# Two attention layers: one head of a pair turned on TensorE instead of by DMA, averages two steps behind their scores

## The chip, the cores and the metric

The kernel runs on one core of a Trainium2 chip. The metric is the device time of one execution in microseconds (us). One core has five engines with instruction streams of their own: PE (TensorE, matrix products), DVE (VectorE), ACT (ScalarE), POOL (GpSimd) and SP (SyncE, which here only issues DMAs). They meet through semaphores. SBUF is the on-chip memory, PSUM the memory of eight banks that PE writes its results to; DRAM is off the core and is reached by DMA.

## What is computed

The input x holds 8 batches of 512 tokens of 256 numbers, f32. Four layers follow, each with a layer norm ahead and added to x:

```
x = x + attention_a(layernorm(x))   # 16 heads of 64, causal, linear bias by distance (alibi), bias on the output
x = x + experts(layernorm(x))       # f1: 8 experts, the best 2 of each token, swiglu
x = x + attention_b(layernorm(x))   # 8 heads of 128, causal, rotary positions
x = x + experts(layernorm(x))       # f2: the same weights as f1
```

Attention is the usual one: scores S = q kT, softmax by rows, then the average of v with the rows of the softmax, and the output projection. In layer b the scores are divided by 128.

```python
sim = jnp.einsum('bhid,bhjd->bhij', q, k) + rel * slopes      # layer a
sim = jnp.where(causal, mask_value, sim)
attn = jax.nn.softmax(sim, axis=-1)
out = jnp.einsum('bhij,bhjd->bhid', attn, v)
return out.reshape(b, n, HEADS * DIM_HEAD) @ w_out + b_out
```

## The kernel before

The order of the whole program is: layer a, expert layer f1, layer b, expert layer f2. Each layer of attention has 64 *steps* (b, g), 8 batches by 8. In layer a a step is a pair of heads (i = 0 and 1, 64 rows of the array each); in layer b it is one head of 128. Tokens are cut in four tiles of 128, and since attention is causal a head's scores are ten blocks of 128x128 (tile `it` of the queries against tiles `jt` up to `it`), which lie packed in one buffer S of 1280 columns (`PACKED`); the layout of the blocks is `S_AT`.

What a step does, with the names that profile rows carry:

- `project` (L334): q (j = 0) and k (j = 1) of the *next* step, on PE, `pp`. In layer a ACT copies q and DVE copies k out of PSUM into `qk`. In layer b positions are rotated: three operations on DVE (`rot`, `rot`, `qk`, L353 to L355) and an add on POOL (L356).
- `scores` (L362): q kT on PE into PSUM, `sp`, in three groups of tiles (n = 0, 1, 2); DVE adds the bias or mask and finds each row's maximum (L413), ACT takes the exponential and its sums (L423). S is left in SBUF. In layer a POOL prepares the two heads' biases, `ali` (L382).
- `send` (L435), right after the last scores: the rows are scaled by 1/sum (L447, on DVE or POOL). The average needs S with keys on the partitions, so S is turned by DMA. The DMA's transpose works on 16-bit numbers: the f32 words are first taken apart in two planes of halves, `apart` (two copies, L450 to L454, on ACT or POOL), these go to DRAM, `away` (640 KB, L456), and a transposing DMA brings them back as `PT` (L460). All of these DMAs are issued from SP's queue.
- `values` (its matmuls are L325): v of two heads at a time, in the even steps, in two pieces `vp`; ACT copies them.
- `average` (L466): the turned blocks against v on PE, `op`, 12 matmuls for each head. It reads `PT`, so it waits for the transpose. Its result goes to `O` (DVE in layer a, ACT in b).
- `project_out` (L498): the output projection of four steps' `O`, `yp`, two pieces in step 5 and two in step 1 of the next batch; DVE adds to x.

`step` (L513) sets the order of these on PE. In layer a: scores 0, 1, 2 of the current step, q of the next step, extras 1, k of the next step, extras 2, then the average of the step before. In layer b: scores 0, q of the next step, scores 1 and 2, k of the next step, extras 1 and 2, then the average of the step before. The extras (L1151 to L1177) are the values, the output projections and small parts of the next layers: the norms (`xn`, `hn`), their transposes on PE (`xtp`, L282), and the gates and counts of the experts (`lp`, `cp`). They fall on fixed g: values on even g, output projections on 1 and 5, the transposes for the expert layer on 3 and for the next batch on 6; g 7 has none.

PE's instructions run in the order in which the program writes them (a manual schedule, L125). The other engines' orders are chosen by the framework's planner. Buffers come from rotating pools, which set who must wait: S has 3 buffers, `PT` 2, `apart` 2, `qk` 3, `tmp` (`ali` and `rot`) 2, the eight PSUM banks are one pool `ps`. `PT`, `apart`, `xT` and S buffers are used again by the expert layers, for gathered rows (`g_f`, L930), activations (L991) and for rows to be added (`collect`, L1105).

Between layers: `layer` (L1141) hands back the work that is left when the 64 steps are done: the average of step 63, the last output projections and the last norm. `flush` (L1195) places these pieces between the first blocks of the expert layer, at the block numbers of `turns`. An expert block is a gather by indirect DMA from POOL's queue (L937), four transposes (`gtp`), the two products (`hp`, `y`) and a scatter (L1041).

Of the kernel before, what the change touches and what calls it, by code (L numbers as in the profile page):

```python
# [49 lines left out]
P = 128  # L50
NB, T, D = 8, 512, 256
NT = T // P
# [15 lines left out]
S_BANKS = [(3,), (2, 0), (1,)]  # L68
BLOCKS_ROW = 10
PACKED = BLOCKS_ROW * P  # L70

AVERAGE = [((0, 1), 0), ((1,), 1), ((2, 3), 0), ((2, 3), 1), ((2, 3), 2), ((3,), 3)]

# [25 lines left out]
def layers(  # L99
# [187 lines left out]
    class Attention:  # L287
# [147 lines left out]
        def send(self, b, g):  # L435

            kind, nh = self.kind, self.nh

            last = (b, g) == (NB - 1, NQ - 1)
            sent = []  # L440
            for i, (S, nm, sums) in enumerate(self.S.pop((b, g))):
                key = f"{kind}_{b}_{g}_{i}"
                nc.vector.reciprocal(sums, sums)
                for it in (3, 2, 0, 1):
                    s = S[:, S_AT[it] * P : (S_AT[it] + it + 1) * P]
                    eng = nc.vector if it == 3 or i == 1 or last else nc.gpsimd
                    eng.tensor_scalar(s, s, sums[:, it : it + 1], 1.0, ALU.mult, ALU.mult)  # L447
                halves = S.bitcast(U16).rearrange("p (w s) -> p s w", s=2)
                apart = work.tile([P, 2, PACKED], U16, tag="apart", name=f"apart_{key}")
                nc.scalar.copy(apart[:, 0, :], halves[:, 0, :])  # L450
                if i == 1 and not last:
                    nc.gpsimd.tensor_copy(apart[:, 1, :], halves[:, 1, :])
                else:
                    nc.scalar.copy(apart[:, 1, :], halves[:, 1, :])  # L454
                away = dram.tile([P, 2, PACKED], U16, tag="away", bufs=4, name=f"away_{key}")
                nc.sync.dma_start(out=away, in_=apart)  # L456
                sent.append(away)
            for i, away in enumerate(sent):
                PT = work.tile([P, PACKED], F32, tag="PT", name=f"PT_{kind}_{b}_{g}_{i}")
                nc.sync.dma_start_transpose(  # L460
                    out=PT.bitcast(U16).rearrange("p (n w) -> p n w", n=BLOCKS_ROW),
                    in_=away.rearrange("p s w -> (p s) w"),
                )
                self.PT[b, g, i] = PT

        def average(self, b, g):  # L466
            kind, nh = self.kind, self.nh
            key = f"{kind}_{b}_{g}"
            PT = [self.PT.pop((b, g, i)) for i in range(nh)]
            if g % HALF == 0:  # L470
                self.O[b] = work.tile(
                    [P, HALF, T], F32, tag="O", bufs=1, name=f"O_{kind}_{b}_{g}"
                )
            v = self.V[b, g // 2]
            op = ps.tile([P, T], F32, tag="ps", bufs=8, name=f"op_{key}")
            cols = P // nh
            for its, jt in AVERAGE:
                n = len(its)
                first = S_AT[its[0]] + jt
                step = S_AT[its[-1]] - S_AT[its[0]] if n > 1 else 1  # L480
                for i in range(nh):
                    c0 = (g % 2) * P + i * cols
                    rows = PT[i].rearrange("p (n w) -> p n w", n=BLOCKS_ROW)
                    nc.tensor.matmul(  # L484
                        op[i * cols : (i + 1) * cols, its[0] * P : (its[-1] + 1) * P].rearrange(
                            "p (n w) -> p n w", n=n
                        ),
                        lhsT=v[:, jt, c0 : c0 + cols],
                        rhs=rows[:, first : first + step * (n - 1) + 1 : step, :],
                        start=(jt == 0),  # L490
                        stop=(jt == its[-1]),
                    )
            if kind == "a":
                nc.vector.tensor_copy(self.O[b][:, g % HALF, :], op)  # L494
            else:
                nc.scalar.copy(self.O[b][:, g % HALF, :], op)
# [13 lines left out]
                    )  # L510
                nc.vector.tensor_tensor(X[b][:, t, :], yp[:, 0:D], X[b][:, t, :], ALU.add)

        def step(self, last, cur, after, extra):  # L513

            there = set(self.qk)

            def project(j):
                if after and (*after, j) not in there:
                    self.project(*after, j)

            self.scores(*cur, 0)
            if self.kind == "a":
                self.scores(*cur, 1)
                self.scores(*cur, 2)
                project(0)
                extra(1)
                project(1)
                extra(2)
            else:
                project(0)  # L530
                self.scores(*cur, 1)
                self.scores(*cur, 2)
                project(1)
                extra(1)
                extra(2)
            if last:
                self.average(*last)


    class Experts:  # L540
# [389 lines left out]
        def gather(self, i, j):  # L930
            m = FIRST[i] + j
            if m % ROWS == 0:
                tag = "apart" if m else "xT"
                self.rows[m // ROWS] = work.tile(
                    [P, ROWS, D], F32, tag=tag, name=f"g_{self.kind}_{m}"
                )
            nc.gpsimd.indirect_dma_start(  # L937
                out=self.rows[m // ROWS][:, m % ROWS, :],
                out_offset=None,
                in_=self.h_all[0 : STAGES[i][1] * T, :],  # L940
                in_offset=bass.IndirectOffsetOnAxis(ap=self.R["token"][i][:, j : j + 1], axis=0),
            )
# [30 lines left out]
        def first(self, i, j):  # L973
# [17 lines left out]
            m = FIRST[i] + j  # L991
            if self.followed and m >= TOTAL - 5:
                if m == TOTAL - 5:
                    self.ended = work.tile([P, 5, FI], F32, tag="PT", name=f"a_{key}")
                a = self.ended[:, m - TOTAL + 5, :]
            else:
                if m % 2 == 0:
                    self.acts = work.tile([P, 2, FI], F32, tag="qk", bufs=3, name=f"a_{key}")
                a = self.acts[:, m % 2, :]
# [105 lines left out]
        def collect(self, b, tiles, tag, engines):  # L1105

            m = b * NT + tiles[0]
            bufs = {"S": 3, "xT": 2, "PT": 2, "apart": 2}[tag]
            got = work.tile(
                [P, 2, len(tiles), D],  # L1110
                F32,
                tag=tag,
                bufs=bufs,
                name=f"yg_{self.kind}_{b}_{tiles[0]}",
            )
            for k in range(2):
                self.read(engines[k], b, got[:, k], k * PLANE + m * P, len(tiles) * P)
            self.got[b, tiles[0]] = got
# [22 lines left out]
    def layer(att, exp, more):  # L1141
# [38 lines left out]
        for n, cur in enumerate(steps):  # L1180
            def extra(k, cur=cur):
                for piece in todo.get((*cur, k), ()):
                    piece()

            att.step(
                steps[n - 1] if n else None,
                cur,
                steps[n + 1] if n + 1 < len(steps) else None,
                extra,
            )  # L1190
        last = steps[-1]

        return [lambda: att.average(*last)] + left

    def flush(left, exp):  # L1195

        turns = (6, 6, 6, 7, 9, 12, 14, 16, 18)
        aside = {}
        for n, piece in zip(turns, left, strict=True):
            aside.setdefault(n, []).append(piece)  # L1200
        for n, piece in zip((20, 22, 24, 26, 29, 32), exp.sorting(1), strict=True):
            aside[n] = [piece]
        return aside
# [17 lines left out]
    aside = flush(layer(att_a, exp_a, more), exp_a)  # L1221
    aside.setdefault(8, []).append(weights_b)
    aside[done] = [lambda: exp_a.fetch(0)]
    for k, tag in enumerate(("xT", "PT")):
        tt = (2 * k, 2 * k + 1)
        aside[done].append(lambda tt=tt, tag=tag: exp_a.collect(0, tt, tag, both_queues))
        aside[done + 3 + k] = [lambda tt=tt: exp_a.add(0, tt)]
# [28 lines left out]
    halves = [(b, tt) for b in range(*STAGES[0]) for tt in ((0, 1), (2, 3))]  # L1256
    for k, (b, tt) in enumerate(halves):
        n = done + 3 * k // 2
        tag = ("xT", "PT")[k % 2] if k not in (8, 9) else "apart"
        aside.setdefault(n, []).append(  # L1260
            lambda b=b, tt=tt, tag=tag: exp_b.collect(b, tt, tag, both_queues)
        )
        aside.setdefault(n + 4, []).append(lambda b=b, tt=tt: exp_b.add(b, tt))
        aside.setdefault(n + 6, []).append(lambda b=b, tt=tt: store(b, tt, nc.sync))
# [1 line left out]
    exp_b.run(aside)  # L1266
    last = [(b, tt) for b in range(*STAGES[1]) for tt in ((0, 1), (2, 3))]
    for k, (b, tt) in enumerate(last):
        exp_b.collect(b, tt, "S" if k < 3 else "apart", (nc.sync, nc.scalar))
    for m in range(end, n + 7):  # L1270
        for piece in aside.get(m, ()):
            piece()
# [69 lines left out]
```

## Time and profile before

| what | value |
|---|---|
| median of 3 runs | 2282.01 us (2281.39 to 2282.07) |
| profiled execution | 2285.09 us |
| its span in the profile | 2283.0 us |
| mean granted clock of PE | 0.964 |
| instructions | 31747 |
| layer a | 16 to about 930 us |
| expert layer f1 alone | about 937 to 1190 us |
| layer b | about 1190 to 2015 us |
| expert layer f2 and the end | to 2283 us |
| DMA queue of SP | 319.28 MB, 51.6% of the 16 DMA engines' span |

The profile is of one execution, 3.1 us slower than the median of the runs, which carry no profiler's records. In its rows "L484 PE MATMUL op_a<-PT_a,V_a x24" means: line 484, engine PE, writes `op_a`, reads `PT_a` and `V_a`, 24 instructions; a bracket at the end says how long the engine was idle just before and what ended it. SPq is the queue of SP. The granted clock of PE is 1.00 at full speed; where it is 0.5 for a stretch, matmuls take twice as long.

### The profile page before, as it was taken

The page shows a single profiled execution, that of the slowest core. Times are in us where ns is not written, and L with a number is a line of the kernel's source. Part 1 is how long each engine was busy: PE and PEld are TensorE (multiplying, and loading weights), DVE is VectorE, ACT ScalarE, POOL GpSimd, SP SyncE. Part 2 cuts the span into 40 slices and gives each one's busy share as a digit, 9 for nine tenths or more (in the row PEclk, how much of TensorE's full clock was granted, in tenths as well). Part 3 has the DMA queues.
Part 4 walks back from the last instruction along what each step waited for, and adds up shares of the span by engine and source line. Part 5 has one row for each costly group of instructions (what it writes and reads, how often), then busy time and mean ns, then how long its engine had stood idle before and what let it go on. Part 6 is the DMA issues. An engine that isn't in the chain of part 4 may idle for free.

```text
span 2283.0 us, 31747 instructions
## 1 busy us (share of the span) xinstructions
PE 2064.2 (90%) x9329; PEld 1332.0 (58%) x9329; DVE 1615.2 (71%) x4943; ACT 1120.8 (49%) x2593; POOL 958.8 (42%) x1211
## 2 busy tenths in 40 slices
PE   6898999999999999799998999999999998989995
PEld 3555555555555555455655666666666665655663
DVE  3466767676767688477676676777677778867768
ACT  3566666666666666323324444444444444432331
POOL 4343434343434333366643343333334333345662
PEclk8999999999999999899999999999999999999998
DMA  9877777878777878732224444454535443452237
GB/s 297 237 191 206 194 205 195 212 195 211 187 212 192 215 182 233 180 109 79 84 77 118 113 141 118 125 144 115 149 105 149 110 135 93 134 147 95 84 100 248
DMA packets 603689, 360.37 MB, mean 158 GB/s; under 512 B 510304, under 2 KB 564736, under 8 KB 603520
## 3 DMA queue, kind: packets, MB, share of 16 engines
q1 hardware_dynamic: 587968, 319.28, 51.6%
q0 software_dynamic: 13632, 37.24, 5.2%
q10 hardware_dynamic: 1920, 1.84, 0.3%
q8 instruction: 77, 1.26, 0.2%
q14 instruction: 92, 0.75, 0.1%
HBM read 67.02 MB, written 165.43 MB: 102 GB/s over the span
## 4 chain that ended last, share of the span: by engine, by line
PE 44%; DVE 8%; DMA 4%; POOL 1%; issue 1%; SPq 1%; ACT 0%; DVEq 0%; another core or an unknown queue 0%; POOLq 0%; ACTq 0%
PE hp_f L980 9%; PE pp_b L343 8%; PE op_b L484 6%; PE sp_b L401 5%; PE yp_b L504 5%; PE y_f L1029 4%; PE vp_b L325 3%; DMA PT_b<-away_b 2%; PE gtp_f L951 1%; PE atp_f L1015 1%; DVE rot_b L354 1%; DVE rot_b L353 1%; DVE S_b L413 1%; DVE qk_b L355 1%; DVE u_f L1001 1%
## 5 line engine op out<-in xcount | busy, mean ns | idle before, releaser
L423 ACT ACTIVATE S_a<-S_a,nm_a 128x512 f32<-128x512 f32 (+3 forms) x512 | 281.0, 552 | 241.1 <-DVE nm_a L413 241.0
L356 POOL TENSOR_TENSOR qk_b<-qk_b,rot_b 128x512 f32<-128x512 f32 x128 | 168.8, 1319 | 394.1 <-DVE qk_b L355 369.8
L484 PE MATMUL op_a<-PT_a,V_a 128*64 128x256 f32 (+1 forms) x1536 | 197.0, 385 | 82.7 <-DMA PT_a<-away_a 79.0
L382 POOL TENSOR_SCALAR ali_a<-alibi 128x512 f32<-128x512 f32 x128 | 79.2, 621 | 433.4 <-DVE nm_a L413 412.8
L423 ACT ACTIVATE S_b<-S_b,nm_b 128x512 f32<-128x512 f32 (+3 forms) x256 | 142.0, 556 | 228.8 <-DVE nm_b L413 228.8
L980 PE MATMUL hp_f<-we,hT_f 128*128 x512 | 246.3, 604 | 7.2 <-DVE u_f L1001 5.8
L413 DVE CUSTOM_DVE_ANT_0 S_a<-sp_a,ali_a 128x512 f32<-128x512 f32 (+3 forms) x512 | 216.7, 487 | 29.9 <-PE sp_a L401 26.8
L484 PEld LDWEIGHTS op_a<-PT_a,V_a 128*64 128x64 f32 x1536 | 122.1, 151 | 169.0 <-DMA PT_a<-away_a 63.8
L484 PE MATMUL op_b<-PT_b,V_b 128*128 128x256 f32 (+1 forms) x768 | 166.5, 371 | 45.6 <-DMA PT_b<-away_b 45.6
L413 DVE CUSTOM_DVE_ANT_0 S_b<-sp_b,mask 128x512 f32<-128x512 f32 (+3 forms) x256 | 115.0, 486 | 127.7 <-PE sp_b L401 127.6
L1041 POOL DMA_INDIRECT y_f<-y_f,row_f x142 | 142.8, 1006 | 144.1 <-DVE y_f L1040 89.7
L450 ACT COPY apart_a<-S_a 128x1280 uint16<-128x1280 uint16 x128 | 161.0, 1258 | 83.6 <-POOL S_a L447 81.1
L1002 ACT ACTIVATE u_f<-u_f 128x256 f32<-128x256 f32 x142 | 59.4, 418 | 266.1 <-DVE u_f L1001 182.0
L484 PEld LDWEIGHTS op_b<-PT_b,V_b 128*128 128x128 f32 x768 | 144.9, 206 | 74.6 <-issue 40.0
L401 PE MATMUL sp_b<-qk_b,qk_b 128*128 128x512 f32 (+3 forms) x512 | 162.1, 440 | 17.3 <-POOL qk_b L356 17.3
L937 POOL DMA_INDIRECT g_f<-h_all_f,token_f x142 | 141.9, 999 | 78.6 <-issue 38.3
L1001 DVE TENSOR_TENSOR u_f<-hp_f,be 128x512 f32<-128x512 f32 x142 | 98.2, 691 | 98.1 <-PE hp_f L980 35.6
L494 DVE COPY O_a<-op_a 128x512 f32<-128x512 f32 x64 | 44.1, 689 | 172.7 <-PE op_a L484 172.6
L401 PE MATMUL sp_a<-qk_a,qk_a 64*128 64x512 f32 (+3 forms) x1024 | 157.8, 447 | 7.0 <-DVE qk_a L360 6.8
L1029 PEld LDWEIGHTS y_f<-we,aT_f 128*128 128x128 f32 x568 | 108.0, 192 | 78.5 <-issue 60.5
L1029 PE MATMUL y_f<-we,aT_f 128*128 x568 | 147.7, 383 | 4.2 <-ACT aT_f L1020 4.0
L447 DVE TENSOR_SCALAR S_a<-S_a,sum_a 128x512 f32<-128x512 f32 (+3 forms) x323 | 141.5, 487 | 4.1
(204 smaller groups left out, 4446.9 us busy)
## 6 DMA issues: line engine op xcount, KB each, us to landing
away_a<-apart_a SPq DMA_DIRECT2D x128, 640.0 KB
away_b<-apart_b SPq DMA_DIRECT2D x64, 640.0 KB
h_all_f<-hn_f SPq DMA_DIRECT2D x64, 128.0 KB
xm_f<-x_mid_f SPq DMA_DIRECT2D x16, 512.0 KB
yg_f<-y_f SPq DMA_DIRECT2D x32, 256.0 KB
yg_f<-y_f SPq DMA_DIRECT2D x56, 128.0 KB
we<-w_dram SPq DMA_DIRECT2D x8, 512.0 KB
x_mid_f<-x SPq DMA_DIRECT2D x8, 512.0 KB
```

Of the source, the lines that this page charges most:

```text
L343: nc.tensor.matmul(pp, lhsT=w[:, c, g * P : (g + 1) * P], rhs=self.xT[b][:, c, :], start=(c == 0), stop=(c == NC - 1),)
L356: nc.gpsimd.tensor_tensor(qk, qk, rot, ALU.add)
L401: nc.tensor.matmul(sp[i][:, at[it] : at[it] + w], lhsT=q[r, it * P : (it + 1) * P], rhs=k[r, 0:w], start=True, stop=True,)
L413: nc.vector.tensor_tensor_reduce(out=s, in0=sp[i][:, at[it] : at[it] + w], in1=add[i][:, T - w : T], scale=scale, scalar=float(np.finfo(np ...
L423: nc.scalar.activation(s, s, AF.Exp, bias=nm[:, it : it + 1], scale=-1.0, accum_out=sums[:, it : it + 1],)
L447: eng.tensor_scalar(s, s, sums[:, it : it + 1], 1.0, ALU.mult, ALU.mult)
L450: nc.scalar.copy(apart[:, 0, :], halves[:, 0, :])
L484: nc.tensor.matmul(op[i * cols : (i + 1) * cols, its[0] * P : (its[-1] + 1) * P].rearrange("p (n w) -> p n w", n=n), lhsT=v[:, jt, c0 : c0 ...
L937: nc.gpsimd.indirect_dma_start(out=self.rows[m // ROWS][:, m % ROWS, :], out_offset=None, in_=self.h_all[0 : STAGES[i][1] * T, :], in_offs ...
L980: nc.tensor.matmul(hp, lhsT=h[:, c * P : (c + 1) * P], rhs=we_sb[:, bass.DynSlice(wat + c * 2 * FI, 2 * FI)], start=(c == 0), stop=(c == N ...
L1029: nc.tensor.matmul(yp, lhsT=aT[:, c * P : (c + 1) * P], rhs=we_sb[:, bass.DynSlice(wat + NC * 2 * FI + c * D, D)], start=(c == 0), stop=(c ...
L1041: made = nc.gpsimd.indirect_dma_start(out=self.y_all, out_offset=bass.IndirectOffsetOnAxis(ap=self.R["row"][i][:, j : j + 1], axis=0), in_ ...
```

## The change

1. *Layer a, head 1 of each pair* is no longer turned by DMA. `send` scales its rows and leaves them in S. One step later a new function, `turn`, turns its ten blocks on PE into three PSUM banks (`tp`: 4, 4 and 2 blocks), from which ACT copies them into a `PT` buffer in a layout of its own (`P_AT`). `average` uses that layout for head 1. Head 0 is turned by DMA as before. Layer b has one head for each step, which is turned by DMA as before.
2. *Averages come two steps behind their scores* in both layers (`older`, step n-2), and earlier in the step: after q of the next step. In layer a the order is now: scores 0 to 2, q, average of n-2, turn of n-1, extras 1, k, extras 2. In layer b: scores 0 to 2, q, average of n-2, k, extras 1 and 2.
3. *Engines:* three of head 1's four scalings go from DVE to POOL. The second copy of halves of head 0 goes from ACT to POOL (both layers); of the two copies for head 1 neither is left.
4. *Buffers:* `PT` 3 in place of 2, `apart` 1 in place of 2. The expert layers' gathered rows lie in `PT` buffers in place of `apart`; the buffers of some `collect`s are changed to fit.
5. *Ends of the layers:* `flush` gets two more pieces. The average of step 62 is at block 0, the turn of step 63 (layer a only) at block 2, the average of step 63 at block 6 as before.

```diff
+P_AT = {0: 0, 1: 4, 3: 7, 2: 8}
+P_BANKS = [(0,), (1, 3), (2,)]
@@ send
-            for i, (S, nm, sums) in enumerate(self.S.pop((b, g))):
+            for i, (S, nm, sums) in enumerate(self.S[b, g]):
...
-                    eng = nc.vector if it == 3 or i == 1 or last else nc.gpsimd
+                    eng = nc.vector if it == 3 or last else nc.gpsimd
                     eng.tensor_scalar(s, s, sums[:, it : it + 1], 1.0, ALU.mult, ALU.mult)
+                if i == 1:
+                    continue
...
-                apart = work.tile([P, 2, PACKED], U16, tag="apart", name=f"apart_{key}")
+                apart = work.tile([P, 2, PACKED], U16, tag="apart", bufs=1, name=f"apart_{key}")
                 nc.scalar.copy(apart[:, 0, :], halves[:, 0, :])
-                if i == 1 and not last:
+                if last:
+                    nc.scalar.copy(apart[:, 1, :], halves[:, 1, :])
+                else:
                     nc.gpsimd.tensor_copy(apart[:, 1, :], halves[:, 1, :])
-                else:
-                    nc.scalar.copy(apart[:, 1, :], halves[:, 1, :])
...
+        def turn(self, b, g):
+            i = 1
+            key = f"{self.kind}_{b}_{g}_{i}"
+            S = self.S.pop((b, g))[i][0]
+            PT = work.tile([P, PACKED], F32, tag="PT", bufs=3, name=f"PT_{key}")
+            self.PT[b, g, i] = PT
+            for n, bank in enumerate(P_BANKS):
+                tp = ps.tile([P, T], F32, tag="ps", bufs=8, name=f"tp_{key}_{n}")
+                base = P_AT[bank[0]]
+                for jt in bank:
+                    for it in range(jt, NT):
+                        o = (P_AT[jt] - base + it - jt) * P
+                        at = (S_AT[it] + jt) * P
+                        nc.tensor.transpose(tp[:, o : o + P], S[:, at : at + P], ident)
+                width = sum(NT - jt for jt in bank) * P
+                nc.scalar.copy(PT[:, base * P : base * P + width], tp[:, 0:width])
@@ average
+                    if i == 1:
+                        first, step = P_AT[jt] + its[0] - jt, 1
@@ step
-            self.scores(*cur, 0)
-            if self.kind == "a":
-                self.scores(*cur, 1)
-                self.scores(*cur, 2)
-                project(0)
+            for n in range(len(S_BANKS)):
+                self.scores(*cur, n)
+            project(0)
+            if older:
+                self.average(*older)
+            if last and self.nh > 1:
+                self.turn(*last)
                 extra(1)
                 project(1)
-                extra(2)
             else:
-                project(0)
-                self.scores(*cur, 1)
-                self.scores(*cur, 2)
                 project(1)
                 extra(1)
-                extra(2)
-            if last:
-                self.average(*last)
+            extra(2)
@@ gather
-                tag = "apart" if m else "xT"
+                tag, bufs = ("PT", 3) if m else ("xT", 2)
@@ layer, at its end
-        return [lambda: att.average(*last)] + left
+        ends = [lambda: att.average(*steps[-2])]
+        if att.nh > 1:
+            ends.append(lambda: att.turn(*steps[-1]))
+        else:
+            ends.append(lambda: None)
+        return ends + [lambda: att.average(*steps[-1])] + left
@@ flush
-        turns = (6, 6, 6, 7, 9, 12, 14, 16, 18)
+        turns = (0, 2, 6, 6, 6, 7, 9, 12, 14, 16, 18)
```

## The prediction

> **What bounds the kernel now.** I read the table of engines first.
>
> ```profile
> PE 2064.2 (90%) x9329; PEld 1332.0 (58%) x9329; DVE 1615.2 (71%) x4943; ACT 1120.8 (49%) x2593; POOL 958.8 (42%) x1211
> ```
>
> PE is the engine with the least room, and the change gives it more to do. So the question is how much of PE's time is not work. The windows of three batches of layer a (span, then each engine, granted clock, DMA share) say:
>
> ```profile
> 252.00:365.30 113.30, 103.64 (x549) 63.98 (x547) 75.80 (x268) 73.52 (x172) 43.43 (x62) 0.97 0.77 200
> 365.30:478.50 113.20, 102.83 (x554) 63.51 (x555) 76.50 (x269) 74.75 (x173) 43.42 (x62) 0.98 0.78 202
> ```
>
> A batch takes 113.2 us, PE idles about 10 of them, and the DMA engines are busy three quarters of the time. PE's groups with the longest idle time name the wait:
>
> ```profile
> L484 PE MATMUL op_a<-PT_a,V_a 128*64 128x256 f32 (+1 forms) x1536 | 197.0, 385 | 82.7 <-DMA PT_a<-away_a 79.0
> ...
> L484 PE MATMUL op_b<-PT_b,V_b 128*128 128x256 f32 (+1 forms) x768 | 166.5, 371 | 45.6 <-DMA PT_b<-away_b 45.6
> ```
>
> Both layers' averages wait for transposes done by DMA. PE's timeline shows one step of layer a; each row is a run of one matmul, and times from start to start are what PE spends on it:
>
> ```profile
> 407.61 1.93 PE L401 MATMUL sp_a<-qk_a,qk_a 64*128 64x512 f32 x14
> 409.47 1.98 PE L343 MATMUL pp_a<-xT_a,wq_a 128*128 128x512 f32 x4
> 411.29 1.04 PE L282 MATMUL xtp_f<-ident,hn_f 128*128 128x128 f32 x8
> 412.16 1.88 PE L343 MATMUL pp_a<-xT_a,wk_a 128*128 128x512 f32 x4
> 415.34 0.62 PE L484 MATMUL op_a<-PT_a,V_a 128*64 128x256 f32 x2 [1.29 <-DMA PT_a<-away_a]
> 417.60 3.68 PE L484 MATMUL op_a<-PT_a,V_a 128*64 128x256 f32 x22 [1.64 <-DMA PT_a<-away_a]
> ```
>
> The average is the last thing in its step and stops twice, once for each head: 1.29 and 1.64 us. The last 22 matmuls then take 3.6 us until 421.21 where the same 22 take 2.3 at 434.47: the granted clock is 0.5 for 3.4 us there, as about twice in each batch. SP's queue shows the two transposes of one step:
>
> ```profile
> 409.04 6.49 SPq L460 DMA_TRANSPOSE PT_a<-away_a  x2
> ```
>
> Three us each, one after the other, and the data land some 2 us later. That is the cause of both stops.
>
> **Layer a, one step at full clock.** From start to start: scores 2.36, each projection 1.82 or 1.72, average 2.31, values 1.72 a piece, output projection 3.45 a piece (440.96 to 444.41). *Added on PE:* 10 transposes. The row nearest is the 8 transposes of 128x128 f32 above, 411.29 to 412.16: 0.109 each, so 1.09 a step and 8.7 a batch. *Added on ACT:* three copies from PSUM; two V copies of 128x512 took 1.06, so about 1.4 a step. *Removed:* one transpose (3.0 of SP's queue), one away (0.5) and two copies of halves (1.25 each; one more goes from ACT to POOL). POOL gets three scalings of head 1, 1.94 (row of head 0's three), and drops nothing but a copy that another replaces. Per step ACT then has 4.4 of exps + 1.26 + 1.4 + 0.58 + up to 1.06 = 8.7, POOL 1.32 + 1.94 + 1.94 + 1.25 = 6.4, DVE about 8.3: all under the shortest step, 9.3. So layer a stays bound by PE.
>
> *The waits.* An average of step n-2 runs in step n. Its DMA chain (scales, halves, away, one transpose) ended 1 to 3 us late; it now has a whole step, 9 to 16 us, more and half the transposes ahead of it. I cost its wait at nothing; the cover is that step, and a transpose must come over 9 us late to be seen. What is late next: the average no longer stands between the second projection and the next scores. DVE's copy of k (0.68, after the matmul's end) was under the average; in steps with nothing behind the projection, g 3 and 7, it is bare, about 1.0 a step. Step 2 adds 0.4, step 6 keeps its three waits of 0.3 for xn. The sum over the eight steps: 12.7 + 16.2 + 13.0 + 11.2 + 13.3 + 16.3 + 13.7 + 10.3 = 106.7, against 113.2. I allow 0.7 for windows of half clock (1.7 lost in each; the idle stretches before them shrink, and it is not certain that the windows go). That is **-5.8 a batch**; bounds +1.0 (the stalls of 8 go, the transposes' 8.7 are paid in full, the half-clock windows stay) and -6.5.
>
> *Batch 0.* Its second step takes 26.3: PE idles 4.2 for a V copy, 6.04 and 2.67 for DMA, and runs slow between. The average(0) that waits there moves one step on, where its data are there. 122.6 should become about 107: **-15** (-8 to -19). *Batches 1 to 6:* 6 x 5.8 = **-35** (+6 to -39). *Batch 7:* **-4** (0 to -5).
>
> *The end of layer a.*
>
> ```profile
> 914.20 2.43 PE L401 MATMUL sp_a<-qk_a,qk_a 64*128 64x512 f32 x16
> 929.06 1.08 PE L484 MATMUL op_a<-PT_a,V_a 128*64 128x256 f32 x2 [12.43 <-DMA PT_a<-away_a]
> ```
>
> Average 62 comes at once after scores 63, waits 12.43 for transposes that ran beside the loads of layer b's weights, and POOL's gathers wait 18.75 for the away behind it, with another 2.4 on PE. After: average 61 and turn 62 stand here, 3.4 us of ready work; average 62 has one transpose and more lead, and the gathers' rows lie in PT buffers that are free after average 61. Of the 15 us lost I take **-11** (-5 to -14; the loads are still there).
>
> **Layer b.** It has one head, so nothing is turned on PE. What changes: averages two steps behind, all scores first, one copy of halves from ACT to POOL (1.25), one apart buffer. The rows of one step:
>
> ```profile
> 1332.52 1.88 PE L343 MATMUL pp_b<-xT_b,wk_b 128*128 128x512 f32 x4
> ...
> 1334.24 1.04 PE L282 MATMUL xtp_f<-ident,hn_f 128*128 128x128 f32 x8
> ...
> 1338.38 4.09 PE L484 MATMUL op_b<-PT_b,V_b 128*128 128x256 f32 x12 [3.10 <-DMA PT_b<-away_b]
> ...
> 1338.86 1.27 POOL L356 TENSOR_TENSOR qk_b<-qk_b,rot_b 128x512 f32<-128x512 f32 x1
> ```
>
> From the second projection's end to the next scores there is a chain: DVE 0.70 + 0.70 + 0.69 and POOL 1.27, with the hand-overs 3.8. Today the average (2.17) and the extras lie over it; after, only the extras do. A bare step is scores 2.16 + 1.72 + 2.17 + 1.72 = 7.77 of PE and 3.8 of chain, 11.55. With values (3.45) 11.55 too, output projections 14.7 (6.91 cover it), step 6 about 13. So: 11.55 + 14.7 + 11.55 + 12.0 + 11.8 + 14.8 + 13.0 + 11.55 = 101.0, and one window of half clock, 1.7, 102.7. Now: 11.9 + 14.7 + 11.2 + 13.9 + 12.0 + 14.8 + 13.5 + 10.5 = 102.5. The wait for DMA (36.7 in the layer's waits) goes and a wait for qk of the same size comes: **0** for batches 1 to 7, bounds -2.3 and +2 each (7 x: -16 and +14). Batch 0 loses 6.4 and 3.4 to its first averages today: **-5**. The end of layer b: average 62 waits 8.92 for its transposes at 2005.6 to 2014.5; the step of lead takes most: **-7** (-4 to -9).
>
> **Sum.** -15 - 35 - 4 - 11 + 0 - 5 - 7 = -77. The profiled execution took 2285.1 (span 2283.0 and 2.1 around it); 2285.1 - 77 = 2208. The median of the runs is 3.1 under the profiled one: **2205**. All terms at their good ends give -107, 2175; all at their bad ends -2, 2280.
>
> **A rule against the change.** The 8 transposes took 0.87 us, in rows of 273 ns each that overlap. The Trainium skill, TensorE: Matmul & The Clock Gate, Part 4: PE-mode transpose, gives about 275 ns for one 128x128 in a kernel (of bf16), and says that transposes do not count as busy time for the clock and that a copy out of PSUM follows. By it ten would cost 2.75 a step, an estimate of 176 us for the layer where the row gives 70, and the sum would turn into a loss of some 30. The row agrees with 275 as the length of one and not as its pace. On the clock, the expert stage (1020 to 1200) has transposes in each block of 3.0 us and a granted clock of 1.00.
>
> **Rivals.**
> 1. *The gain is mostly paid away*: 2235 to 2277. Half-clock windows stay, the transposes cost their full 8.7 a batch and layer b loses 1 or 2 a batch to the bare chain; what is left are the ends and batch 0, -15 - 11 - 5 - 7 = -38 or less: 2243. For it: PE has only 8 us of recorded DMA wait per batch of layer a, less than the transposes added. Against: 17 us of each batch are not full-clock work.
> 2. *Slower: POOL's queue in layer b.* Per step it holds scales 1.7, the copy 1.3, q's add 1.27 and k's add 1.27, in this order. Today scales start 5.9 after the second scores do (1331.22 to 1337.16), 2.1 of it DVE's work for q, which now comes later; with all scores first that is 4.7 from the step's start, and I take 5.3. Then q's add ends at 9.5, and k's is due at 10.1: 0.6 to 0.9 of room. If scales or copy come later than that (DVE beside POOL slows: 1.35 for an operation that takes 0.48 alone; the copy waits until the one apart buffer is sent), each us of it is a us of each of some 40 steps. From 2 us on it eats the 77: 13.5 instead of 11.55; with 2.5, 2302. Against: the away of the step before lands some 7 us ahead of the copy.
> 3. *Clock*: gaps of 3.8 in 16 steps of b and of 1 in layer a make new windows of half clock, 1.7 each; 45 of them (33 now) would cancel the gain.
> 4. *The layers run ideal*: under 2180.
>
> **Chances.** Forecast (2180 to 2235) 0.52; rival 1 0.22 (some of it within 0.2%); rival 4 0.08; slower by 2 or 3, 0.18, mostly under 2310. Range 2172 to 2275: what is left out is most of rival 2 and 3 and the ideal end of 4. Faster by over 0.2% (4.6 us; about what a measurement of this kernel can tell from no change) 0.79, within it 0.03, slower 0.18.
>
> **What would show it.** In the changed profile: the wait of op_a for DMA all but gone (now 79.0); transposes of S at 0.11 apiece; DMA share in layer a down from 0.77 to about half; batches of 106 to 108 in a and 101 to 104 in b; sp_b's wait for POOL qk_b up from 16 to between 50 and 70, in g 3 and 7 above all (2.9 and 3.8 each). Wrong would be: transposes at 0.27, sp_b waiting in every step, the granted clock under 0.95 in layer a, op_a waiting for ACT's copies of PT or scores waiting for a buffer of S that POOL holds.

## The result: no change, where 3.4% less was forecast

The changed kernel took 2283.69 us (median of 20 runs, 2271.43 to 2288.10), the kernel before 2282.05 (20 runs, 2275.30 to 2287.37). The ratio is 0.9999 (95% interval 0.9985 to 1.0012). Forecast were 2205 and a range of 2172 to 2275. A second comparison (`after_again` below) gave 0.9970 (0.9949 to 0.9991): a third of a per cent, half of one at most.

Yet much has moved inside. The profiled executions took 2285.09 and 2285.50, so their stretches can be laid side by side. They are read off PE's timeline, from the start of a step's first scores (`sp`) to another's; the last block's product is the last run of `y`:

| stretch | before | after | difference | forecast |
|---|---|---|---|---|
| start to first scores of a | 16.4 | 15.3 | -1.1 | 0 |
| layer a, first to last scores | 897.8 | 879.3 | -18.5 | -54 |
| last scores of a to first of b | 276.5 | 264.1 | -12.4 | -11 |
| layer b, first to last scores | 812.5 | 837.9 | +25.4 | -5 |
| last scores of b to the last block's product | 256.1 | 256.2 | +0.1 | -7 |
| from there to the end | 23.7 | 31.0 | +7.3 | 0 |

Some 32 us were gained up to layer b, and given back in layer b and in the last 30 us.

**Layer a.** Of the page after the change, PE's average of layer a:

```profile
L506 PE MATMUL op_a<-PT_a,V_a 128*64 128x256 f32 (+1 forms) x1536 | 155.5, 350 | 4.0 <-ACT PT_a L484 3.8
```

The wait for DMA, 79.0 before, is gone; what is left waits for `turn`'s copy. The windows of two batches (span, busy time of PE, PEld, DVE, ACT, POOL, then granted clock, DMA share, GB/s):

```profile
252.00:365.00 113.00, 109.65 (x656) 71.03 (x653) 70.60 (x250) 67.94 (x189) 55.18 (x89) 1.00 0.38 108
365.00:478.00 113.00, 109.65 (x644) 71.53 (x643) 70.44 (x247) 67.08 (x181) 55.91 (x91) 1.00 0.40 108
```

The clock is whole and the DMA share has halved, both as forecast. But PE is busy 109.65 of 113: the room that the stalls left has been largely filled by the transposes. PE's timeline of the step g 2 shows what remains:

```profile
383.76 1.88 PE L346 MATMUL pp_a<-xT_a,wk_a 128*128 128x512 f32 x4
385.48 1.89 PE L328 MATMUL vp_a<-wv_a,xT_a 128*128 128x256 f32 x8
388.97 2.43 PE L404 MATMUL sp_a<-qk_a,qk_a 64*128 64x512 f32 x16 [1.60 <-DVE qk_a L363]
391.33 1.99 PE L346 MATMUL pp_a<-xT_a,wq_a 128*128 128x512 f32 x4
393.25 2.38 PE L506 MATMUL op_a<-PT_a,V_a 128*64 128x256 f32 x24
395.56 1.31 PE L482 MATMUL tp_a<-ident,S_a 128*128 128x128 f32 x10
```

Ten turns take 1.15 from start to start (395.56 to 396.71), and the scores wait 1.60 for k's copy on DVE, behind DVE's work for the expert layer's norm, although values lie between.

**Layer b.** Of the same page, the scores of layer b, and two steps of PE's timeline, g 3 and 7:

```profile
L404 PE MATMUL sp_b<-qk_b,qk_b 128*128 128x512 f32 (+3 forms) x512 | 180.2, 502 | 73.1 <-POOL qk_b L359 73.1
```

```profile
1412.03 1.88 PE L346 MATMUL pp_b<-xT_b,wk_b 128*128 128x512 f32 x4
1413.74 1.04 PE L285 MATMUL xtp_f<-ident,hn_f 128*128 128x128 f32 x8
1418.31 4.09 PE L404 MATMUL sp_b<-qk_b,qk_b 128*128 128x512 f32 x8 [3.53 <-POOL qk_b L359]
...
1465.60 1.88 PE L346 MATMUL pp_b<-xT_b,wk_b 128*128 128x512 f32 x4
1471.15 2.42 PE L404 MATMUL sp_b<-qk_b,qk_b 128*128 128x512 f32 x8 [3.66 <-POOL qk_b L359]
```

The wait for qk went from 17.3 to 73.1, while the wait of `op_b` for DMA, 45.6 before, is no longer in the list of waits. The first scores after the gap took 3.93 to the next start where others take 2.16: PE had a granted clock of 0.5. In the records half clock lasts 79 us between the first and last scores of layer b, 44 before. This is the window of that stretch before the change, its clock third from the right (0.95 after it, in a window shown with `b_fill3`):

```profile
1190.70:2003.20 812.50, 752.36 (x3035) 519.96 (x3033) 599.64 (x1641) 377.94 (x777) 306.66 (x387) 0.97 0.45 125
```

The chain behind the gap, from the timeline of all engines:

```profile
1467.59 0.69 DVE L356 TENSOR_TENSOR rot_b<-pp_b,sin 64x512 f32<-64x512 f32 x1 [1.08 <-POOL apart_b L458]
1468.30 0.68 DVE L357 TENSOR_TENSOR rot_b<-pp_b,sin 64x512 f32<-64x512 f32 x1
1469.00 0.69 DVE L358 TENSOR_TENSOR qk_b<-pp_b,cos 128x512 f32<-128x512 f32 x1
1469.83 1.26 POOL L359 TENSOR_TENSOR qk_b<-qk_b,rot_b 128x512 f32<-128x512 f32 x1 [1.03 <-DVE qk_b L358]
```

k's projection ends at 1467.48 (1465.60 + 1.88), its rotated form at 1471.09 (1469.83 + 1.26), and PE has nothing between. The bracket of the first row names POOL's copy of halves, which ended within 0.1 us of the projection; `b_copy_act` below tells the two apart.

**The end.** The last fetches in SP's queue and DVE's last additions, before the change:

```profile
2267.26 1.98 SPq L1086 DMA_DIRECT2D yg_f<-y_f  x4
```

```profile
2263.77 15.33 DVE L1126 SCALAR_TENSOR_TENSOR xm_f<-yg_f,wt_f,xm_f 128x256 f32<-128x256 f32 x33
```

After the change:

```profile
2253.05 7.32 SPq L1268 DMA_DIRECT2D out_dram<-xm_f  x4
2261.09 5.24 SPq L1104 DMA_DIRECT2D yg_f<-y_f  x6
```

```profile
2257.66 5.98 DVE L1144 SCALAR_TENSOR_TENSOR xm_f<-yg_f,wt_f,xm_f 128x256 f32<-128x256 f32 x13
...
2270.72 0.49 DVE L1144 SCALAR_TENSOR_TENSOR xm_f<-yg_f,wt_f,xm_f 128x256 f32<-128x256 f32 x1 [7.09 <-DMA yg_f<-y_f]
```

Where SP issued four fetches of `yg`, it now issues six: two that belong to the first six batches stand behind the four that must wait for the last block's scatter. DVE, which added without a break until 2279.1 (2263.77 + 15.33), now idles 7.09.

### The profile page after: what moved, and what is told of

The parts are those of the page before. It is cut to its first block, busy times and chain, and to the rows that moved or that the text cites. A ratio compares the mean times of both kernels' runs of the same rounds, so it can differ in the third digit from the quotient of the medians.

```text
span 2283.7 us, 32906 instructions
## 1 busy us (share of the span) xinstructions
PE 2106.3 (92%) x9969; PEld 1377.7 (60%) x9969; DVE 1579.2 (69%) x4754; ACT 980.2 (43%) x2594; POOL 1103.5 (48%) x1463
## 4 chain that ended last, share of the span: by engine, by line
PE 41%; DVE 11%; POOL 7%; issue 3%; DMA 1%; another core or an unknown queue 1%; ACT 0%; DVEq 0%; POOLq 0%; SPq 0%; ACTq 0%
PE hp_f L998 9%; PE sp_b L404 6%; PE pp_b L346 6%; PE yp_b L526 5%; PE y_f L1047 4%; PE op_b L506 3%; POOL qk_b L359 3%; DVE rot_b L357 2%; POOL apart_b L458 2%; DVE rot_b L356 2%; PE vp_b L328 1%; POOL S_b L449 1%; PE gtp_f L969 1%; PE atp_f L1033 1%; DVE qk_b L358 1%
## 5 line engine op out<-in xcount | busy, mean ns | idle before, releaser
L449 POOL TENSOR_SCALAR S_b<-S_b,sum_b 128x384 f32<-128x384 f32 x189 | 96.7, 529 | 355.7 <-DVE sum_b L445 355.6
L404 PE MATMUL sp_b<-qk_b,qk_b 128*128 128x512 f32 (+3 forms) x512 | 180.2, 502 | 73.1 <-POOL qk_b L359 73.1
L449 POOL TENSOR_SCALAR S_a<-S_a,sum_a 128x384 f32<-128x384 f32 x378 | 201.3, 547 | 35.6 <-DVE sum_a L445 34.6
L404 PEld LDWEIGHTS sp_b<-qk_b,qk_b 128*128 128x128 f32 x512 | 96.6, 218 | 150.7 <-POOL qk_b L359 89.4
L356 DVE TENSOR_TENSOR rot_b<-pp_b,sin 64x512 f32<-64x512 f32 x128 | 88.7, 693 | 117.5 <-PE pp_b L346 63.1
L506 PEld LDWEIGHTS op_b<-PT_b,V_b 128*128 128x128 f32 x768 | 137.4, 192 | 43.3 <-issue 23.5
L506 PE MATMUL op_a<-PT_a,V_a 128*64 128x256 f32 (+1 forms) x1536 | 155.5, 350 | 4.0 <-ACT PT_a L484 3.8
L506 PEld LDWEIGHTS op_a<-PT_a,V_a 128*64 128x64 f32 x1536 | 100.9, 137 | 90.9 <-ACT S_a L426 28.1
```

Of the source, the lines that this page charges most:

```text
L356: nc.vector.tensor_tensor(rot[0:h], pp[h:P], sin_sb[h:P], ALU.mult)
L404: nc.tensor.matmul(sp[i][:, at[it] : at[it] + w], lhsT=q[r, it * P : (it + 1) * P], rhs=k[r, 0:w], start=True, stop=True,)
L506: nc.tensor.matmul(op[i * cols : (i + 1) * cols, its[0] * P : (its[-1] + 1) * P].rearrange("p (n w) -> p n w", n=n), lhsT=v[:, jt, c0 : c0 ...
```

## The experiments

The theory after the first look: layer a's gain is real, and layer b's new order gives it back, through k's bare chain and the half clock that its gaps bring. Rivals: the copy of halves in POOL's queue, the lead of two steps, the smaller buffers. With the changed layer a, the stretch from layer a to b took from 250 to 271 us in different runs, and the chip alone doesn't say which (chip 7 showed 251 and, later, 271). So each ratio is against the kernel before, run beside it, and across runs only the stretches of the layers a and b are compared. The edits are shown shortened, some with lines joined by `;`.

**Layer a alone, layer b alone.** `a_only`: layer b has its old order, lag and copies.

```diff
+            if self.kind == "b":
+                self.scores(*cur, 0); project(0); self.scores(*cur, 1); self.scores(*cur, 2)
+                project(1); extra(1); extra(2)
+                if last: self.average(*last)
+                return
```

> Layer a as changed; layer b with its old order, averages one step behind and both copies of halves on ACT; buffers and the end as changed. In the profiles, the changed kernel is 32 us ahead when layer b's first scores start, loses 25 between the first and the last scores of layer b, and 7 after the last expert block. Theory (the order in layer b gives the gain back): layer b's stretch is 812 again within 8 (838 in the changed kernel), and the whole 2250 to 2264. Rival (what layer a gains is lost later in any case, whatever layer b does): 2276 or more.

Measured: ratio 0.9907 (0.9876 to 0.9937); layer b 813.0, layer a 881.7. As the theory had it, some 20 us below the kernel before. (The whole, 2239.35, is under the 2250 expected, since the kernel before took 2258.66 beside it.)

`b_only`: the kernel before with the changed order of b and its POOL copy, all buffers as they were.

```diff
+            if self.kind == "b":
+                for n in range(len(S_BANKS)): self.scores(*cur, n)
+                project(0)
+                if older: self.average(*older)
+                project(1); extra(1); extra(2)
+                return
...
-                if i == 1 and not last:
+                if (i == 1 or kind == "b") and not last:
```

> Layer a and all buffers as before; layer b alone with all scores first, averages two steps behind and ahead of k, the second copy of halves on POOL. Theory (the order in layer b costs 25): the stretch of layer b 830 to 845, the whole 2300 to 2315. Rival (layer b loses only through the smaller buffers, one for apart and three shared for PT): the stretch stays near 812, and the whole 2275 to 2288.

Measured: 1.0084 (1.0056 to 1.0112), some 20 us more; layer b 825.1 where at least 830 was expected, wait for qk 72.8. The order costs with the old buffers too, though the stretch is 13 shorter than in the changed kernel's first profile (55 us of half clock, not 79). A gain of 0.9% and a loss of 0.8% make the 1.000.

**Is it the copy on POOL?** `b_copy_act` takes it back to ACT:

```diff
-                if last:
+                if last or kind == "b":
                     nc.scalar.copy(apart[:, 1, :], halves[:, 1, :])
```

> As changed, but in layer b the second copy of halves is on ACT again. Rival POOL: layer b falls to 820 or less, the whole to 2266 or less. Theory (order): k's chain is as bare as it was, in g 3 and 7; layer b 830 to 838, the whole 2275 to 2284.

Measured: 1.0023 (1.0009 to 1.0038), layer b 841.7, wait for qk 67.2. In this order it is not the copy.

**Is it only that the average stands ahead of k?** `b_split`:

```diff
+            if self.kind == "b":
+                self.scores(*cur, 0); project(0); self.scores(*cur, 1); self.scores(*cur, 2)
+                project(1)
+                if older: self.average(*older)
+                extra(1); extra(2)
+                return
```

> As changed, but in layer b scores 0, q, scores 1 and 2, k, then the average of two steps back, then the extras: k is again ahead of the average, which covers k's way through DVE and POOL. Theory (order): the wait for DMA stays away and the wait for qk falls from 73 to 20 or less; layer b 765 to 795, the whole 2215 to 2243. Rival POOL (the copy of halves in POOL's queue, and one apart buffer, are what delays the scores): the wait for qk stays above 50 and layer b above 820, the whole 2265 or more. Rival lag (two steps behind costs by itself): layer b 812 or more, 2257 or more.

Measured: 0.9935 (0.9912 to 0.9957), layer b 819.1, wait for qk 61.2. **Here the theory fell in its simple form**: the cover was back and the scores still waited. Half clock was 48 us in place of 79; counting half of that as lost (an estimate), it makes 15 of the 19 us gained on 838. The timeline at the end of a step g 7 says why:

```profile
1446.77 0.66 DVE L358 TENSOR_TENSOR qk_b<-pp_b,cos 128x512 f32<-128x512 f32 x1
1446.95 1.56 POOL L449 TENSOR_SCALAR S_b<-S_b,sum_b 128x384 f32<-128x384 f32 x3 [1.41 <-DVE sum_b L445]
...
1448.48 1.26 POOL L359 TENSOR_TENSOR qk_b<-qk_b,rot_b 128x512 f32<-128x512 f32 x1
...
1449.79 1.13 PE L404 MATMUL sp_b<-qk_b,qk_b 128*128 128x512 f32 x2 [2.62 <-POOL qk_b L359]
```

Both rotations and the maxima lie on DVE one after the other, then k's add stands in POOL's queue behind the scalings: it starts at 1448.48, 1.05 after the end of DVE's `qk`. That moving the average on PE can't shorten such a step is argued from this row; `b_two_ahead` moves the chain instead. `b_split_act`, this edit and that of `b_copy_act` together:

> As b_split, with the second copy of halves on ACT as before the change. In b_split the add of k stood ahead of that copy in POOL's queue and behind the scalings. Theory (DVE's and POOL's work for q, k and the rows is the bound of the bare steps, not this copy): layer b 812 to 825, wait for qk 50 to 65. Rival POOL (the copy): layer b 800 or less, wait for qk under 35.

Measured (one run, no interval): layer b 805.4, wait for qk 56.2: 14 us for the copy in this order, some 3 of them through half clock (41 us in place of 48), between the two expectations; the chain remains. This run differs from `a_only` only in the averages, one step further behind and ahead of the extras: 805.4 against 813.0, with 41 us of half clock in both. So with the chain in its place the lead was worth some 8 us.

**Taking the chain off the path.** `b_two_ahead`: q and k of step n+2 right after the average in step n (at g 7 the next batch's first two steps), 4 buffers of qk in place of 3, 6 of the 1 KB buffers in place of 8.

```diff
+                for n in range(len(S_BANKS)):
+                    self.scores(*cur, n)
+                ahead(after)              # what is still missing of the next step
+                if older:
+                    self.average(*older)
+                ahead(far)                # q and k of step n + 2
+                extra(1)
+                extra(2)
```

> As changed, but in layer b q and k are made two steps ahead of their scores (4 buffers of qk, one step's projections right after the average; at g 7 two steps' worth), so that their way through DVE and POOL has a whole step. Buffers of 1 KB for norms 6 in place of 8, to make room. The runs before showed that neither k ahead of the average (wait for qk still 61) nor the copy on ACT (67) frees layer b alone. Theory (the chain of q and k through DVE and POOL is the bound of the bare steps, and its gaps bring the half clock): wait for qk under 15, layer b 740 to 780 from 838, ratio to the kernel before 0.955 to 0.978. Rival (DVE has too much work in all, 9.1 us a step, wherever the chain lies): layer b 805 or more, ratio 0.985 or more.

Measured: 0.9556 (0.9531 to 0.9581); layer b 734.5 with 10 us of half clock, 103 us less than in the changed kernel's first profile (90 less than the 825 that other runs show); a middle batch 92.5 in place of 105 to 107. PE's waits in layer b:

```profile
PE inv_f L915 <- DVE col_f L900: 10.0, 3, 7.2
PE yp_b L526 <- ACT O_b L518: 0.7, 1, 0.7
PE op_b L506 <- DMA PT_b<-away_b: 0.7, 2, 0.4
PE sp_b L404 <- POOL qk_b L359: 0.6, 1, 0.6
```

The scores and averages wait for nothing any more. DVE's work is the same (613.8 us in 734.5, 617.0 in 837.9): it had never been too much, only too late.

**Is the lead of the averages worth anything, then?** `b_ahead_lag1`:

```diff
-                if older:
-                    self.average(*older)
                 ahead(far)
                 extra(1)
                 extra(2)
+                if last:
+                    self.average(*last)
```

> b_two_ahead with layer b's averages one step behind again, as the last thing in the step. Tells whether the change's own aim in layer b, the lead for the DMA, is worth anything once the chain of q and k is off the path. Theory (before, the wait for the DMA lay beside that chain and its removal bought little; without the chain it is the bound): waits of op_b for DMA 80 us or more, layer b 790 to 825 from 735. Rival (the DMA is early enough in any case): waits under 45, layer b 760 or less.

Measured: 0.9690 (0.9654 to 0.9727), layer b 758.5, wait of `op_b` for DMA 23.0 in all, 11.6 of it between the first and last scores. Both numbers lie where the rival had them, under 45 and under 760: the DMA is nearly early enough in any case. Still the lead is worth 24 us with the chain gone, where it was worth some 8 with the chain in place.

**The half clock.** `b_fill` puts matmuls whose result nobody reads into the gap, at the end of g 3 and 7:

```diff
+            if self.kind == "b" and after and cur[1] in (3, 7):
+                fill = ps.tile([P, T], F32, tag="ps", bufs=8, name=...)
+                for n in range(7):        # b_fill3: 3
+                    nc.tensor.matmul(fill, lhsT=wk[:, 0, 0:P], rhs=self.xT[after[0]][:, 0, :], ...)
```

> As changed, with seven idle-time matmuls of 128x512 (3.0 us, their results not used) on PE at the end of steps g 3 and 7 of layer b, in the gap where PE waits 3.5 us for k. Theory (a gap of 3.5 us is what brings half clock into the next step): half clock in layer b falls from 79 us to under 35, layer b from 838 to 805 to 822. Rival (half clock comes from something else): half clock over 60 us, layer b 832 or more.

Measured: 0.9992 (0.9980 to 1.0005), layer b 838.1, half clock 10 us in place of 79. The clock did as the theory said and the time did not, because the filler was twice as long as planned:

```profile
1412.28 6.17 PE L559 MATMUL fill<-xT_b,wk_b 128*128 128x512 f32 x14
```

Seven f32 matmuls are 14 instructions of 0.43. So `b_fill3`:

> As b_fill, with three matmuls in place of seven. In b_fill one f32 matmul of 512 columns took 0.86 us, not 0.43, so seven took 6.0 and were themselves what the next scores waited for: half clock fell to 10 us but steps g 3 and 7 became 14.8 and 13.8. Three take 2.6 and fit into the gap of 3.5. Theory (the gaps bring the half clock, which costs layer b some 35 us): half clock in layer b under 30 us, steps g 3 and 7 at 12.4 and 11.6 as in the changed kernel, layer b 803 to 815, ratio to the kernel before 0.983 to 0.991. Rival (it takes more than a busy PE in the gap): layer b 830 or more.

Measured: 0.9854 (0.9834 to 0.9874), layer b 809.4, half clock 14 us. The windows of the whole stretch, changed kernel and `b_fill3` (the last three figures are the clock, the DMA share and GB/s):

```profile
1158.60:1996.50 837.90, 764.25 (x3022) 519.89 (x3021) 616.99 (x1638) 303.49 (x714) 375.57 (x450) 0.95 0.43 121
```

```profile
1147.10:1956.50 809.40, 774.60 (x3112) 522.65 (x3111) 616.49 (x1638) 302.45 (x714) 374.89 (x450) 0.99 0.46 125
```

Steps g 3 and 7 are 12.4 and 11.6 in both, and g 0 and 4 fall from as much as 14.8 to 11.7 and 12.1. Useless work makes the layer 28 us shorter than in the changed kernel's first profile. `tail` below, on the same chip and with layer b as changed, has 824.4 and 55 us of half clock; against it the gain is 15. That is the gaps' second price.

**Layer a.** `a_k_first` projects k right after q, ahead of average and turn:

```diff
                 project(0)
+                project(1)
                 if older: self.average(*older)
                 if last: self.turn(*last)
                 extra(1)
-                project(1)
                 extra(2)
```

> As changed, but in layer a k is projected right after q, ahead of the average and the turn. Theory (what layer a gained less than forecast is in part k's bare copy, 22 to 24 us of waits of the scores for DVE's qk): that wait falls under 8, layer a from 880 to 855 to 866, ratio 0.985 to 0.994. Rival (the time turns up as another wait, for ACT's copies of PT or for the extras): layer a 874 or more, ratio 0.997 or more.

Measured: 0.9854 (0.9822 to 0.9885); layer a 849.1 (under the 855 to 866 expected), a batch 107.1 in place of 110.3; the scores wait 1.1 us in all for DVE's qk. g 2 is 1.7 shorter, g 3 and 7 1.0 each, the seventh batch 6.6 in all and the last one 4.0.

`a_dma2` turns both heads by DMA with averages two steps behind; `turn` is not called, and `average` reads both in the old layout:

```diff
-                    eng = nc.vector if it == 3 or last else nc.gpsimd
+                    eng = nc.vector if it == 3 or i == 1 or last else nc.gpsimd
...
-                if i == 1:
-                    continue
```

> As changed, but in layer a both heads are turned by DMA again, with averages two steps behind and the order of the changed kernel; three PT buffers and one apart buffer for both heads; copies and scalings of head 1 as before. Theory (the two steps of lead alone would have hidden the DMA, and the turns on PE, 1.15 a step, are a price of 73 us): layer a 805 to 835, ratio 0.97 to 0.98. Rival (two transposes a step and one apart buffer can't keep up): waits of the averages for PT 40 us or more, layer a 875 or more, ratio 0.997 or more.

Measured: 1.0341 (1.0293 to 1.0388), layer a 956.4. The averages' own wait for DMA is 24.9 us, under the rival's 40. This doesn't settle whether the turn on PE is needed: the two heads share one apart buffer here, and in 120 us of layer a (350 to 470) POOL waits 21.4 and ACT 16.2 for it to be sent, with their queues behind. No run has two such buffers beside three of PT.

**The end.** `tail` gives the late fetch a buffer that is free:

```diff
-        tag = ("xT", "PT", "xT", "apart", "xT", "PT", "xT", "PT", "apart", "PT", "xT", "PT")[k]
+        tag = ("xT", "PT", "xT", "apart", "xT", "PT", "xT", "PT", "PT", "PT", "xT", "apart")[k]
```

> As changed, with the last fetch of the first six batches' rows in the apart buffer, so that SP's queue issues it ahead of the four fetches that wait for the last expert block. Theory (in the changed kernel this fetch stood behind them, and DVE idled 7.1 us at the end): from PE's last product to the end 21 to 22 us as before the change, from 28; ratio 0.9965 to 0.9985. Rival (the end is bound by DMA in any case): 27 or more, ratio 0.9995 or more.

Measured: from the last product to the end 23.6, from 31.0; DVE's row:

```profile
2220.98 15.14 DVE L1144 SCALAR_TENSOR_TENSOR xm_f<-yg_f,wt_f,xm_f 128x256 f32<-128x256 f32 x33
```

The idle time is gone: 7.4 us, as expected. The whole ratio, 0.9907 (0.9879 to 0.9935), is more than that; layer b was 824.4 in this run. So the changed kernel was run again (`after_again`):

> The changed kernel itself, beside the kernel before on one chip once more. In the runs so far the stretch of layer b with the changed order was 838 in some profiles and 824 in others, with 79 and 55 us of half clock: in every batch the gaps are the same, but they bring a window in some batches and none in others. Theory (the windows fall differently from execution to execution or chip to chip): a ratio of 0.994 to 1.002, layer b 824 or 838. Rival (tail's 0.9907 was its own effect): ratio 0.998 to 1.002 and layer b 838.

Measured: the 0.9970 above, layer b 825.0 with 55 us of half clock; so `tail`'s 824.4 is not its own effect. Every other batch takes 102.1 here, where the first profile has 104.8 to 106.8 in all the middle ones, with the same gaps in g 3 and 7. The record says more of this: of twelve executions on this one chip nine took 2284.0 to 2287.8 at a mean granted clock of 0.972 to 0.975, and three 2297.2 to 2298.5 at 0.967 or 0.968. So the time varies by some 13 us between executions on one chip. That the windows in layer b make it is inferred, since only one of the twelve has a profile.

**All three.** `best`: `a_k_first`, `b_two_ahead` and `tail`.

> a_k_first, b_two_ahead and tail together. If the three costs are independent: layer a 849, layer b 735, the end 22; ratio to the kernel before 0.933 to 0.943. If they hide one another (DVE's work under layer a's waits, the DMAs of layer b): 0.95 or more.

Measured: 0.9378 (0.9361 to 0.9395), 2124.53 beside 2265.80 on that chip; layer a 852.8, layer b 734.4, the end 23.1. The gains add up: 1 - 0.0146 - 0.0444 - some 0.003 (7.4 of 2266 us) is 0.938.

## Why the prediction was wrong, step by step

The forecast missed by 79 us. By the profiles, 35 of them lie in layer a, 30 in layer b, 7 at the end of layer b and 7 at the end of the program. Two terms of the sum failed by 25 each: "-5.8 a batch" for batches 1 to 6 of layer a, and "0" for batches 1 to 7 of layer b.

*Waits for DMA in layer a, costed at nothing:* right. *Ten transposes, 1.09:* 1.15 measured; right, and with the turns in every step the granted clock is 1.00 in layer a's middle batches. The Trainium skill (TensorE: Matmul & The Clock Gate, Part 4: PE-mode transpose) gives some 275 ns for one transpose and doesn't count transposes as busy for the clock. As a pace this layer contradicts the 275: 0.115 us each. For the clock it is no test, since other matmuls fill most of each step, 10.5 to 16.6 us. *Batch 0, -15:* -13.6. *The end of layer a, -11:* -12.4.

*Batches 1 to 6, "-5.8 a batch":* -10 in all for -35. The sum of 106.7 was 110.3: k's bare copy was priced at 1.0 in g 3 and 7, rightly, but 0.4 in g 2, where it cost 1.7; the other steps ran 0.2 to 0.5 longer than their parts. With k ahead, `a_k_first` gives the forecast 107. And 113.2, read off two batches, is 112.6 as the mean of the six. *Batch 7, -4:* +5.3. The scores wait there for DVE, which sorts for the expert layer (4.4 for `number_f`, 3.9 for `qk`); that the waits for DMA hid this before is argued, not shown.

*Layer b, "0" for batches 1 to 7:* +25. The chain of 3.8 was right, and a batch's steps came out a little short: 101.0 forecast, 102.1 in `b_fill3`, which has 14 us of half clock in all. **The failed term is "one window of half clock, 1.7"** a batch. As the mean of batches 1 to 6, the first profile has 106.7, `after_again` 104.7 and `b_fill3` 102.7: the windows cost 4.0 a batch in the one and 2.0 in the other. The prediction had this as rival 3 at 1.7 for each new window, and asked for 45 more; there were fewer in all, 23 for 33, but nine of the fourteen in layer b were 6.8 us long (3.4 lost). An estimate that counts half of all half clock as lost puts the stretch without it at 790 before and at 799 and 798 in the two profiles after. By it some 8 us are the bare chain's, and 17 in the first profile or 5 in the second the clock's.

The prediction let a wait for qk take the place of layer b's wait for DMA and so forecast no gain there. That was right in kind: the two lay side by side, and the lead alone is worth some 8 us (`a_only` to `b_split_act`). *Batch 0, "-5":* +0.1.

*The end of layer b, "-7":* 0.1. Average 62 no longer waits 8.92, but the first gather's rows come late (5.65 of wait at 2006.78), and one more average, 2.2, has moved behind the last scores.

*Buffers of the collects:* not priced at all, +7.3. Ahead of the prediction the change of tags is told as "changed to fit"; but a fetch whose buffer comes free late had moved in SP's queue behind four that wait for the end.

*Rival 2, POOL's queue,* the slower side: wrong mechanism for this kernel. POOL idles 1.03 before k's add until DVE's `qk` is there (the chain's last row above), and `b_copy_act` gains nothing; in the step of `b_split` shown above the queue did hold k's add, for 1.05. *Rival 1's* 2243 had the losses too small.

## What to carry to other kernels

Before a wait is removed, ask what else ends at the same moment: here DMA's wait and the q/k chain lay side by side, and removing the first alone bought little. A latency chain over two slow engines is best given a whole step of lead by issuing its producer earlier, rather than covered by moving one piece of PE's work. Price a PE gap like these of 3.5 us twice, for itself and for the clock behind it, and follow every renamed buffer to the queue that waits for it.

## What the runs showed of the hardware

Gaps of 3.5 us on PE were followed by a granted clock of 0.5 for 3.4 or 6.8 us in many steps and not in others; with matmuls in the gap the windows went (79 us to 10 and 14). In the trace of every run here, the windows of half clock start at whole multiples of 3.413 us from one another, and until PE's work ends they last one to four such units. In the changed kernel's layer b, for example, they start at 1363.7, 1418.3 and 1520.7, which are 16 and 30 units apart. So the same gap meets another place of this grid in another batch; that this decides whether it brings a window is inferred, not shown.

In layer a behind its first batch there are 3 us of half clock after the change, where the gaps in most batches are single ones of 0.9 and 1.6, and 41 us before, where two gaps such as 1.29 and 1.64 stood 0.6 us of work apart.

One f32 matmul of 512 columns appears as two instructions of 0.43. By the same count the 12 instructions of one head's average, called 12 matmuls ahead of the prediction, are six matmuls; a turn of one block is one instruction.
